# Another order of work at the end of each layer of a two-layer graph attention kernel

## The chip, the cores and the metric

One core of a Trainium2 chip runs the whole kernel. The metric is the device time of one execution in microseconds (us); less is better. The time before is the median of three runs; one more execution was profiled, and every row quoted here comes from that one. Engines are named as in the profile: PE (TensorE), DVE (VectorE), ACT (ScalarE), POOL (GpSimd) and SP (SyncE). Each engine works through its own list of instructions in order and waits on semaphores for the others.

## The reference, cut to what matters

Two graph attention layers over 6250 nodes with 256 features and 200000 edges, sorted by their destination. Layer 0 has four heads, layer 1 has one. For each layer:

```
te  = relu(edge_attr @ We + be) * exp(x @ Wo + bo)[src]      # edge features
hx  = x @ Wg                                                # node rows
al  = leaky_relu(a_s.hx[src] + a_d.hx[dst] + a_e.(te @ Wge))  # one logit per edge and head
m   = segment_max(al, dst);  p = exp(al - m[dst])
out = segment_sum(p * hx[src], dst) / segment_sum(p, dst) + b
```

Every node also has a loop to itself, whose edge feature is the mean of those that come in. Layer 0 adds its input and a Relu, layer 1 adds its input and the features from ahead of both layers.

## The kernel before, in words

**Tiling.** The edges are cut into 1563 chunks of 128, and these into 66 superchunks per layer: 64 of 24 chunks, then one of 14 and one of 13 (`cuts`, line 47). Edges are sorted, so a superchunk covers at most 112 neighbouring nodes, and its sums are one PSUM tile of 128 rows.

**A superchunk's steps**, with the methods that issue them:

- `gather` (L866): POOL issues one indirect DMA for each chunk (L873), which fetches 128 rows of the layer's node table into G.
- `spread`, `parts`, `blocks` (L981, L1012, L1033): DVE prepares the destination's term of the logits; `blocks` writes the block product aq (L1037).
- `rphase1` (L948) is a generator: for each half of the features PE multiplies (L964) and ACT applies the Relu (L967 or L969). `rphase2` (L978) and `adst` (L1044) add both terms in PSUM (zad); `edge_rows` (L1047) transposes them on DVE.
- `logits` (L1064): DVE adds the gathered terms (L1072 is the first instruction that needs the gathers) and scans for segment maxima (L1087, L1089). `ends` transposes the scans' ends on PE (L1100), `links` (L1102) scans them on DVE (L1110, L1112) and transposes back on PE (L1117).
- `maxima` (L1119): DVE forms the maxima (L1127 to L1147), ACT the Exp (L1146), DVE stores the weights (L1150). `scale` (L1174) multiplies G by them on DVE (L1181). `carried` (L1155) adds the open row of the superchunk before, from its evicted sums U, to G.
- `onehots` (L1001) builds the one-hot matrix S on DVE (L1009). `sums` (L1185) multiplies S and G chunk by chunk on PE (L1193) into u, and `evict` (L1195) copies u to U on ACT (L1198).
- `finish` (L1311): the merge with the loop to itself, `merge` (L1200) and the rest of `nodes0` or `nodes1` (L1246, L1300). It is a generator as well, so its steps can be set singly between others. In layer 1 its last two steps (L1306, L1308) write the result row fb.
- In layer 0 `rows1` (L1286 on PE, L1288 on ACT), `rows2` (L444 on PE) and `rows3` (L448 on DVE, L1298 on ACT, a write by SP, L1327) make layer 1's table row. In layer 1 `rows3` alone writes fb out: by SP (L1332), and by a POOL scatter (L1335) for the last two superchunks.

**Order.** The order of issue is the order in which these methods are called; no scheduler moves them. `edges` (L637) calls them for each superchunk, with the next superchunk's features between. The last three of each layer, called a, b and c here (24, 14 and 13 chunks), are issued by `ending` (L736), once per layer. `pv` is the superchunk ahead of a, `late` the one before that, and `after` the first superchunk of the next layer, or nothing in layer 1. At the end of layer 0, `gather(after)` reads the table that a, b and c have just written; it waits for the last write. Buffers that bound the order: U has three buffers, S, fb and the table row two, u, y and zad in PSUM one each.

Of the kernel before, what the change touches and what calls it, by code (L numbers as in the profile page):

```python
# [32 lines left out]
C = 24  # L33
# [46 lines left out]
class Kernel:  # L80
# [655 lines left out]
    def ending(self, a, b, c, pv, late, after):  # L736

        nc, k = self.nc, a["k"]
        self.load_lb(k + 3)
        self.load_lb(k + 4)  # L740
        self.gather(b)
        self.gather(c)
        for q in () if after else (b, c):
            q["idx"] = idx = self.np_.tile([P, 1], I32, name="oidx")
            nc.vector.tensor_add(idx, self.base_f[:, q["s"]:q["s"] + 1], self.iota_m)
            nc.vector.memset(idx[0:1, :], 1 << 20)
        drain(self.logits(a))
        self.ends(a)
        self.spread(b)
        self.parts(b)  # L750
        y = self.rphase1(b)
        next(y)
        self.links(a)
        self.rows2(late)
        self.load_fl(k + 1)
        self.blocks(b)
        drain(self.maxima(a))
        drain(y)
        self.load_ea(k + 2)
        self.rphase2(b)  # L760
        self.adst(b)
        drain(self.scale(a))
        self.carried(a)
        n = a["C"]
        self.sums(a, (0, n // 2))
        self.rows3(late)
        self.edge_rows(b)
        self.onehots(b)
        drain(self.logits(b))
        self.ends(b)  # L770
        self.rows1(pv)
        self.spread(c)
        self.parts(c)
        self.sums(a, (n // 2, n - n // 4))
        self.links(b)
        self.sums(a, (n - n // 4, n))
        self.load_fl(k + 2)
        self.rows2(pv)
        y = self.rphase1(c)
        next(y)  # L780
        self.blocks(c)
        drain(self.maxima(b))
        self.evict(a)
        drain(y)
        self.load_ea(k + 3)
        self.rphase2(c)
        self.adst(c)
        self.rows3(pv)
        n = b["C"]
        drain(self.scale(b, cuts=(1, 1 + n // 2, n)))  # L790
        drain(self.scale(b, cuts=(0, 1)))
        self.carried(b)
        self.onehots(c)
        f = self.finish(a)
        if after:
            for _ in range(9):
                next(f)
        else:
            drain(f)
            self.rows3(a)  # L800
        m = c["C"]
        self.sums(b, (1, n - 3))
        self.edge_rows(c)
        drain(self.logits(c))
        self.ends(c)
        for _ in range(3):
            next(f, None)
        self.links(c)
        self.sums(b, (n - 3, n), (0, 1))
        self.load_fl(k + 3)  # L810
        drain(f)
        self.evict(b)
        if after:
            self.rows1(a)
            self.rows2(a)
        drain(self.maxima(c))
        y = self.rphase1(after) if after else iter(())
        next(y, None)
        drain(self.scale(c, cuts=(1, 1 + m // 2, m)))
        drain(self.scale(c, cuts=(0, 1)))  # L820
        self.carried(c)
        self.sums(c, (1, m), (0, 1))
        if after:
            self.rows3(a)
        f = self.finish(b)
        while after and "hw" not in b:
            next(f)
        if not after:
            drain(f)
            self.rows3(b)  # L830
        self.evict(c)
        drain(f)
        drain(y)
        self.rows1(b)
        self.rows2(b)
        f = self.finish(c)
        while after and "hw" not in c:
            next(f)
        if after:
            self.rows3(b)  # L840
        drain(f)
        self.rows1(c)
        self.rows2(c)
        self.rows3(c)
        if after:
            self.gather(after)
            self.nodes(after)
            self.spread(after)
            self.parts(after)
            self.blocks(after)  # L850
            self.rphase2(after)
            self.adst(after)
            self.edge_rows(after)
            self.onehots(after)
# [602 lines left out]
def drain(g):  # L1457
    for _ in g:
        pass
# [93 lines left out]
```

## Time and profile before

| what | value |
|---|---|
| median of 3 runs (lowest to highest) | 4082.15 us (4076.27 to 4089.95) |
| profiled execution | 4081.92 us, its span 4080.1 us |
| busy over the span: PE, DVE, ACT, POOL | 3031.4, 2850.5, 520.3, 3008.6 us |
| ending of layer 0, 2009 to 2084 (75 us): PE, DVE, ACT, POOL busy | 53.0, 55.2, 12.6, 23.8 us |
| ending of layer 1, 4009 to 4081 (72 us): PE, DVE, ACT, POOL busy | 40.9, 39.7, 5.1, 26.2 us |

A row of the timeline reads: start in us from the span's start, duration in us, engine, line of the kernel, operation, output<-inputs, partitions x elements, count, and in brackets how long the engine stood idle before it and what ended that. Neighbouring instructions of one line are merged into one row with their count. A row of a source line reads: count, shortest/median/longest duration in ns, first and last start in us. The chain of waits is followed back from the last instruction; its shares are those of the span.

### The profile page before, as it was taken

Reading aid. Unit: us, or ns where it says so; the run is one execution under the profiler, and the core shown is the slowest. Engines: PE = TensorE matmul, PEld = TensorE weight load, DVE = VectorE, ACT = ScalarE, POOL = GpSimd, SP = SyncE. Lnnn points to the kernel's source line nnn. Section 1 sums busy time; section 2 is a strip of 40 time slices with the busy share of each in tenths; the row PEclk is TensorE's granted clock in tenths of the full one; section 3 lists DMA queues with packets and bytes.
Section 4 is the critical chain, followed back from the end, with each engine's and each line's share of the span. In section 5 each row is a group of like instructions: output and inputs, shape, how many; then the busy total and the mean of one; then the engine's idle time right before and its main releaser. Section 6 shows DMA issues by size and latency. Waiting matters only on the chain.

```text
span 4080.1 us, 34027 instructions
## 1 busy us (share of the span) xinstructions
PE 3031.4 (74%) x9878; PEld 1887.7 (46%) x9878; DVE 2850.5 (70%) x6188; ACT 520.3 (13%) x1162; POOL 3008.6 (74%) x3255
## 2 busy tenths in 40 slices
PE   8878778777877878878756767767677677676776
PEld 6555444444444544544534444444444444444444
DVE  7898777877877877778755656656566565665665
ACT  5111111111111111111110000000000000000000
POOL 6677777777777777777747777777777777777774
PEclk9787777777777777877767777777777777777777
DMA  7455555555555555455434454454445445445542
GB/s 254 130 151 140 144 150 142 144 150 139 146 150 140 145 149 147 140 148 148 134 99 131 138 142 134 139 142 140 135 138 140 135 138 144 131 138 143 141 133 81
DMA packets 231086, 576.17 MB, mean 141 GB/s; under 512 B 63098, under 2 KB 87872, under 8 KB 230826
## 3 DMA queue, kind: packets, MB, share of 16 engines
q0 software_dynamic: 150144, 422.75, 38.9%
q1 hardware_dynamic: 80331, 150.52, 11.5%
q8 instruction: 79, 1.29, 0.1%
q14 instruction: 116, 0.94, 0.1%
q10 hardware_dynamic: 416, 0.67, 0.1%
HBM read 542.72 MB, written 31.09 MB: 141 GB/s over the span
## 4 chain that ended last, share of the span: by engine, by line
POOL 33%; DVE 31%; issue 13%; PE 12%; DMA 8%; ACT 2%; DVEq 0%; SPq 0%; ACTq 0%; POOLq 0%
POOL G L873 33%; DVE G L1181 11%; DMA G<-T,src 7%; PE y L964 6%; DVE S L1009 6%; PE u L1193 2%; DVE rt L1058 2%; DVE lb L993 1%; ACT R L969 1%; PE ps L444 1%; PE zad L978 1%; DVE G L1163 1%; DVE ade L1061 1%; DVE al L1076 1%; DVE al L1074 1%
## 5 line engine op out<-in xcount | busy, mean ns | idle before, releaser
L873 POOL DMA_INDIRECT G<-T,src x3102 | 2956.6, 953 | 1010.5 <-issue 912.6
L1193 PE MATMUL u<-G,S 128*128 128x270 f32 (+1 forms) x6252 | 1474.8, 396 | 113.8 <-DVE G L1171 109.2
L1193 PEld LDWEIGHTS u<-G,S 128*128 128x128 f32 x6252 | 1199.2, 194 | 396.0 <-DVE G L1171 172.7
L1181 DVE TENSOR_TENSOR G<-G,kps 128x6144 f32<-128x6144 f32 (+2 forms) x140 | 853.3, 6100 | 0.0
L964 PE MATMUL y<-ea,webd 64*128 64x384 f32 (+1 forms) x1056 | 729.5, 840 | 68.7 <-ACT R L969 66.9
L1100 PE MATMUL lf<-ident,fb 128*36 128x128 f32 (+1 forms) x132 | 49.8, 377 | 674.1 <-DVE fb L1089 647.6
L1072 DVE TENSOR_TENSOR G<-rt,G 128x96 f32<-128x96 f32 (+1 forms) x132 | 30.4, 230 | 715.5 <-DMA G<-T,src 714.8
L978 PE MATMUL zad<-R,wea 128*64 128x384 f32 (+1 forms) x1056 | 469.7, 804 | 1.5 <-ACT R L969 1.2
L964 PEld LDWEIGHTS y<-ea,webd 64*128 64x128 f32 x1056 | 294.3, 307 | 317.2 <-issue 191.3
L1009 DVE TENSOR_TENSOR S<-kps,loc 128x3072 f32<-128x3072 f32 x132 | 437.6, 3315 | 4.6
L969 ACT ACTIVATE R<-y,webd 128x768 f32<-128x768 f32 x260 | 233.2, 897 | 1523.5 <-PE lf L1117 1130.1
L1100 PEld LDWEIGHTS lf<-ident,fb 128*36 128x36 f32 (+1 forms) x132 | 15.6, 118 | 716.1 <-DVE fb L1089 688.7
L978 PEld LDWEIGHTS zad<-R,wea 128*64 128x64 f32 x1056 | 158.2, 206 | 315.9 <-issue 208.7
L1127 DVE TENSOR_TENSOR fb<-flpen,lf 128x192 f32<-128x192 bf16 (+1 forms) x132 | 36.7, 278 | 237.7 <-PE lf L1117 237.7
L1030 PE MATMUL zad<-a,Q 128*128 128x12 bf16 (+1 forms) x132 | 25.8, 196 | 155.8 <-DVE a L1025 155.8
L1058 DVE STREAM_TRANSPOSE rt<-zad 128x768 f32<-128x768 f32 (+1 forms) x130 | 124.8, 960 | 9.5 <-PE zad L1044 8.9
L444 PE MATMUL fin<-wg,h1T 128*128 128x260 f32 x264 | 129.0, 640 | 2.0 <-ACT h1T L1288 2.0
L1198 ACT ACTIVATE U<-u 128x270 f32<-128x270 f32 (+1 forms) x132 | 51.8, 393 | 500.6 <-PE u L1193 500.6
L993 DVE TENSOR_TENSOR lb<-lb,kps 128x1536 bf16<-128x1536 bf16 (+1 forms) x68 | 113.6, 1670 | 0.0
L444 PEld LDWEIGHTS fin<-wg,h1T 128*128 128x128 f32 x264 | 72.4, 302 | 48.3 <-issue 33.9
L1030 PEld LDWEIGHTS <-Q 128*128 128x128 bf16 x132 | 16.0, 121 | 169.2 <-DVE a L1025 162.6
L1223 ACT ACTIVATE mw<-mw,mg 128x2 f32<-128x2 f32 x66 | 19.7, 298 | 576.2 <-DVE mg L1222 576.2
(191 smaller groups left out, 2160.9 us busy)
## 6 DMA issues: line engine op xcount, KB each, us to landing
G<-T,src POOLq DMA_INDIRECT x3102, 2.8
ea<-in_ea_dram SPq DMA_DIRECT2D x64, 768.0 KB
lb<-locrow SPq DMA_DIRECT2D x64, 384.0 KB
T<-t1row SPq DMA_DIRECT2D x66, 227.5 KB
tw<-T SPq DMA_DIRECT2D x66, 225.8 KB
tw<-T SPq DMA_DIRECT2D x66, 117.2 KB
tw<-in_x_dram SPq DMA_DIRECT2D x66, 112.0 KB
out_dram<-fb SPq DMA_DIRECT2D x64, 112.0 KB
```

Source lines behind the costliest of these rows:

```text
L444: self.nc.tensor.matmul(ps[:, :L.MW], hT[:, k, :], self.wg[L.l][:, k, :], start=(k == 0), stop=(k == 1))
L873: nc.gpsimd.indirect_dma_start(out=G[:, c, 0:L.TW], out_offset=None, in_=self.rows[L.l][0:n * (1 + L.l), :], in_offset=bass.IndirectOffset ...
L964: nc.tensor.matmul(y[:, o], self.webd[l][r, :], ea[r, w], start=True, stop=True)
L969: nc.scalar.activation(R[:, i, :32 * c].rearrange("p (b n) -> p b n", b=2), y.rearrange("p (b n) -> p b n", b=2)[:, :, :16 * c], AF.Relu, ...
L978: nc.tensor.matmul(st["zad"][i * PH:(i + 1) * PH, o], self.wea[l][0], R[:, i, w], start=True, stop=False)
L993: V.tensor_tensor(lb[:, :, :n], lb[:, :, :n], self.k_part.unsqueeze(2).to_broadcast([P, i, n]), op=OP.is_equal)
L1009: nc.vector.tensor_tensor(st["S"][:, c0:c1, :], self.k_iota.unsqueeze(1).to_broadcast(w), self.loc[:, o + c0:o + c1].unsqueeze(2).to_broad ...
L1058: V.transpose(rv[:, :32 * c].rearrange("p (b n) -> p b n", b=2), z.rearrange("p (b n) -> p b n", b=2)[:, :, :16 * c])
L1100: self.nc.tensor.transpose(self.lf[0:e.shape[1], 1:P + 1], e, self.ident)
L1181: nc.vector.tensor_tensor(v, v, pw[:, c0:c1, :].unsqueeze(3) .to_broadcast([P, c1 - c0, H, L.F]), op=OP.mult)
L1193: nc.tensor.matmul(st["u"][:, :L.W], S[:, i, :], G[:, i, 0:L.W], start=(j == 0), stop=(j == c - 1))
L1198: self.nc.scalar.activation(U[:, :L.W], st["u"][:, :L.W], AF.Copy)
```

## The change

All of it lies in `ending`, so it acts once in each layer. Nothing is computed otherwise; the instructions are the same in number and shape, and their order changes:

- a's sums are cut after 8 and 12 of 24 chunks instead of after 12 and 18; the transposes of b's logits and of b's links stand at the cuts.
- b's maxima, a's eviction and b's scaling move ahead of c's edge features (`rphase1(c)`, `blocks(c)`). Before, maxima and eviction stood behind the first half of these, the scaling behind all of them.
- a's merge: four steps stay where nine (layer 0) or all (layer 1) stood; three follow behind c's `ends`, one behind the last of b's sums, the rest after c's carried row.
- c's maxima move ahead of b's eviction.
- In layer 0 a's table rows (`rows1`, `rows2`, `rows3`) move from before c's maxima to behind c's eviction. In layer 1 a's result is written after c's sums are issued.

```
         n = a["C"]
-        self.sums(a, (0, n // 2))
+        self.sums(a, (0, n // 3))
...
-        self.sums(a, (n // 2, n - n // 4))
+        self.sums(a, (n // 3, n // 2))
         self.links(b)
-        self.sums(a, (n - n // 4, n))
+        self.sums(a, (n // 2, n))
         self.load_fl(k + 2)
         self.rows2(pv)
+        drain(self.maxima(b))
+        self.evict(a)
+        n = b["C"]
+        drain(self.scale(b, cuts=(1, 1 + n // 2, n)))
+        drain(self.scale(b, cuts=(0, 1)))
         y = self.rphase1(c)
         next(y)
         self.blocks(c)
-        drain(self.maxima(b))
-        self.evict(a)
         drain(y)
         self.load_ea(k + 3)
         self.rphase2(c)
         self.adst(c)
         self.rows3(pv)
-        n = b["C"]
-        drain(self.scale(b, cuts=(1, 1 + n // 2, n)))
-        drain(self.scale(b, cuts=(0, 1)))
         self.carried(b)
         self.onehots(c)
         f = self.finish(a)
-        if after:
-            for _ in range(9):
-                next(f)
-        else:
-            drain(f)
-            self.rows3(a)
+        for _ in range(4):
+            next(f)
         m = c["C"]
         self.sums(b, (1, n - 3))
         self.edge_rows(c)
         drain(self.logits(c))
         self.ends(c)
         for _ in range(3):
-            next(f, None)
+            next(f)
         self.links(c)
         self.sums(b, (n - 3, n), (0, 1))
         self.load_fl(k + 3)
-        drain(f)
+        next(f)
+        drain(self.maxima(c))
         self.evict(b)
-        if after:
-            self.rows1(a)
-            self.rows2(a)
-        drain(self.maxima(c))
         y = self.rphase1(after) if after else iter(())
         next(y, None)
         drain(self.scale(c, cuts=(1, 1 + m // 2, m)))
         drain(self.scale(c, cuts=(0, 1)))
         self.carried(c)
+        drain(f)
         self.sums(c, (1, m), (0, 1))
+        f = self.finish(b)
         if after:
+            while "hw" not in b:
+                next(f)
+        else:
             self.rows3(a)
-        f = self.finish(b)
-        while after and "hw" not in b:
-            next(f)
-        if not after:
             drain(f)
             self.rows3(b)
         self.evict(c)
+        self.rows1(a)
+        self.rows2(a)
         drain(f)
+        if after:
+            self.rows3(a)
         drain(y)
         self.rows1(b)
         self.rows2(b)
```

## The prediction

> **What bounds the kernel now.** I read the page first, for the chain that ended last, then the instructions of the gather line in layer 1.
>
> ```profile
> span 4080.1 us, 34027 instructions
> POOL 33%; DVE 31%; issue 13%; PE 12%; DMA 8%; ACT 2%; DVEq 0%; SPq 0%; ACTq 0%; POOLq 0%
> POOL G L873 33%; DVE G L1181 11%; DMA G<-T,src 7%; PE y L964 6%; DVE S L1009 6%; PE u L1193 2%; DVE rt L1058 2%; DVE lb L993 1%; ACT R L969 1%; PE ps L444 1%; PE zad L978 1%; DVE G L1163 1%; DVE ade L1061 1%; DVE al L1076 1%; DVE al L1074 1%
> L873 POOL DMA_INDIRECT G<-T,src x1563: 942/946/1172, 2083.6 to 4039.9; - x196
> ```
>
> Layer 1 runs from its first gather at 2083.6 to its last at 4039.9: 1563 gathers in 1956.3 us are 1.25 each, which is one gather's 0.95 plus 0.30 of issue. POOL never pauses for long, so all of layer 1 hangs on the moment of its first gather, and what the change saves ahead of it arrives at the end whole. The change touches only the two endings (about 2009 to 2084 and 4009 to 4081), some 3.6% of the span; the other 96% I leave as it is. a, b and c are the last three superchunks (24, 14 and 13 chunks; a chunk's sum is two matmuls). Times are us from the span's start, and "now" is the kernel before.
>
> **Layer 1's ending, up to c's gathers.** The timeline, in order:
>
> ```profile
> 4022.36 7.85 PE L1193 MATMUL u<-G,S 128*128 128x261 f32 x24 [2.99 <-DVE G L1171]
> 4022.36 0.95 POOL L873 DMA_INDIRECT G<-T,src  x1 [0.30 <-issue]
> 4026.41 0.18 DVE L1072 TENSOR_TENSOR G<-rt,G 128x14 f32<-128x14 f32 x1 [1.19 <-DMA G<-T,src]
> 4027.38 0.20 DVE L1089 TENSOR_TENSOR_SCAN fb<-pen,al 128x14 f32<-128x14 bf16 x1
> 4030.18 2.89 PE L1193 MATMUL u<-G,S 128*128 128x261 f32 x12
> 4033.28 0.18 DVE L1127 TENSOR_TENSOR fb<-flpen,lf 128x28 f32<-128x28 bf16 x1 [1.80 <-PE lf L1117]
> 4033.87 0.20 DVE L1140 TENSOR_SCALAR mt<-lf,m 1x1 f32<-1x1 f32 x1
> 4037.08 0.76 ACT L967 ACTIVATE R<-y,webd 128x224 f32<-128x224 f32 x2 [20.00 <-PE y L964]
> 4037.72 0.19 ACT L1146 ACTIVATE kps<-mt 128x15 f32<-128x15 f32 x1
> 4038.03 4.01 DVE L1181 TENSOR_TENSOR G<-G,kps 128x1792 f32<-128x1792 f32 x3
> 4038.78 1.52 PE L978 MATMUL zad<-R,wea 128*64 128x224 f32 x8
> 4039.86 0.95 POOL L873 DMA_INDIRECT G<-T,src  x1 [0.30 <-issue]
> 4040.43 4.59 PE L1193 MATMUL u<-G,S 128*128 128x261 f32 x20
> ```
>
> - The cut of a's sums at 8 chunks instead of 12. b's scan (L1089) is done at 4027.58, but its transpose queues behind 24 matmuls until 4030.2. The last 8 of these run at the pace of the next row (2.89 / 12 = 0.24), so 16 end near 4028.3. The transposes go there; four chunks more (1.9) end at 4030.4, and L1117 lets L1127 start at 4030.7 instead of 4033.28: 2.6 earlier. PE does the same matmuls without a gap, so a's sums end, and c's edge features begin, where they do now.
> - b's maxima and scaling ahead of c's edge features. Now b's Exp (L1146) is ready at 4033.87 + 0.20 = 4034.07, but ACT holds c's first Relu (L967), which waits 20 us for PE; the Exp starts at 4037.72: 3.65 lost. In the new order it follows L1127 by 0.8, at 4031.5, on an idle ACT. Scaling starts 0.31 after it and takes 4.01: 4031.8 to 4035.8 instead of 4042.04.
> - What stands behind it. c's block product (L1037, 0.2) now waits on DVE for that scaling: done at 4036.0. PE first needs it at L978, 4038.78, so 2.7 of slack hides it; without slack each us late would cost one. a's eviction now precedes c's Relu on ACT, at a's last sum (4030.2 and two stretches of 2.9: near 4036.1), and its 0.4 lies under the matmuls of c's first half (the Relu starts at 4037.08). So b's sums start at 4040.43 as now, and ten chunks end at 4045.0. This edit alone is worth nothing on PE; it empties DVE.
> - DVE then: carried row 0.6, one-hots of c 2.0, four steps of a's merge 0.8 (all lengths of now), done near 4040.3; c's transposes and reduce follow its features (4040.7) until 4041.9.
>
> c's logits have to wait for c's own gathers. b shows the lag: last gather 4022.36 + 0.95, logits at 4026.41, 3.1 later. c's last ends at 4040.81, so its logits start at **4043.9**.
>
> **Layer 1's ending, from c's logits on.**
>
> ```profile
> 4048.67 0.18 DVE L1072 TENSOR_TENSOR G<-rt,G 128x13 f32<-128x13 f32 x1 [0.18 <-issue]
> 4049.85 0.42 PE L1100 MATMUL lf<-ident,fb 128*33 128x128 f32 x1 [4.83 <-DVE fb L1089]
> 4051.61 0.18 DVE L1127 TENSOR_TENSOR fb<-flpen,lf 128x26 f32<-128x26 bf16 x1 [0.41 <-PE lf L1117]
> 4054.96 0.39 ACT L1198 ACTIVATE U<-u 128x261 f32<-128x261 f32 x1 [9.04 <-PE u L1193]
> 4055.24 0.18 ACT L1146 ACTIVATE kps<-mt 128x14 f32<-128x14 f32 x1
> 4055.54 3.74 DVE L1181 TENSOR_TENSOR G<-G,kps 128x1536 f32<-128x1536 f32 x3
> 4057.39 7.64 PE L1193 MATMUL u<-G,S 128*128 128x261 f32 x26 [2.47 <-issue]
> 4059.86 0.20 DVE L1214 SCALAR_TENSOR_TENSOR mg<-U,cnt,tw 128x1 f32<-128x1 f32 x1
> 4062.30 0.48 DVE L1308 SCALAR_TENSOR_TENSOR fb<-tw,mw,fb 128x256 f32<-128x256 f32 x1
> 4065.07 0.39 ACT L1198 ACTIVATE U<-u 128x261 f32<-128x261 f32 x1 [4.04 <-PE u L1193]
> 4068.72 1.00 POOL L1335 DMA_INDIRECT out_dram<-fb,oidx  x1 [4.63 <-DVE flag_i L864]
> ```
>
> - Logits: 4048.67 becomes 4043.9, 4.77 earlier. The transpose follows 1.18 later, at 4045.1, just behind b's ten chunks (4045.0). The three steps of a's merge placed here run in PE's shadow; the fourth (L1306, 0.48) overlaps L1117, costing about 0.05. L1127 at 4046.85.
> - c's Exp: 0.8 later, 4047.65. Now it starts at 4055.24, because b's eviction (4054.96) stands ahead of it on ACT; the change swaps them. **7.6 earlier.** Scaling starts at 4047.95 and b's eviction goes beside it.
> - c's sums start at 4057.39 - 7.6 = 4049.8. Their 26 matmuls take 7.64, though 20 took 4.59 before: at 0.22 more for each, 26 are 5.91. The 1.73 between are matmuls on the halved clock after PE stood still for 2.47. In the new order b's last chunks (1.9) end near 4048.5, and the still stretch before c's is 1.3. I take the full pace: the last sum ends at 4055.7, eviction 9.3 earlier than 4065.07. Bounds: 7.6 (as slow as now) to 9.3; I take **9.3**.
> - DVE's queue in that stretch: c's scaling to 4051.7, carried row 0.55, the rest of a's merge (L1308, 0.5), then b's merge (4059.86 to 4062.78: 2.9) to 4055.7, just when U of c arrives (4056.1). It is hidden by 0.4; if c's sums got faster yet, b's merge would be next. SP's write of a goes out at 4052.8 instead of 4047.7 and POOL's scatter of b at 4055.8; in this ending neither queue has anything behind them but c's scatter. From c's eviction to the last scatter (4068.72) and the end nothing is changed.
>
> **Layer 0's ending.** The same steps with four heads, then the tables of layer 1:
>
> ```profile
> 2046.28 5.27 PE L1193 MATMUL u<-G,S 128*128 128x270 f32 x20
> 2054.90 0.40 PE L1100 MATMUL lf<-ident,fb 128*36 128x128 f32 x1 [3.35 <-DVE fb L1089]
> 2056.26 0.42 DVE L1266 TENSOR_TENSOR fa<-tw,mw 128x256 f32<-128x256 f32 x1
> 2058.76 0.26 DVE L1127 TENSOR_TENSOR fb<-flpen,lf 128x104 f32<-128x104 bf16 x1
> 2061.31 0.22 ACT L1146 ACTIVATE kps<-mt 128x56 f32<-128x56 f32 x1
> 2061.69 3.74 DVE L1181 TENSOR_TENSOR G<-G,kps 128x1536 f32<-128x1536 f32 x3
> 2064.02 6.19 PE L1193 MATMUL u<-G,S 128*128 128x270 f32 x26
> 2070.25 0.40 ACT L1198 ACTIVATE U<-u 128x270 f32<-128x270 f32 x1 [1.47 <-PE u L1193]
> 2072.96 1.15 PE L444 MATMUL fin<-wg,h1T 128*128 128x260 f32 x4 [0.89 <-ACT h1T L1288]
> 2076.07 0.42 ACT L1272 ACTIVATE fb<-fb 128x256 f32<-128x256 f32 x1 [1.26 <-DVE fb L1270]
> 2077.76 2.10 PE L444 MATMUL fin<-wg,h1T 128*128 128x260 f32 x4 [0.53 <-ACT h1T L1288]
> 2083.62 0.94 POOL L873 DMA_INDIRECT G<-T,src  x1 [43.94 <-DMA T<-t1row]
> ```
>
> - b's ten chunks end at 2051.55. By the steps of layer 1, half a us longer for four heads, DVE has c's scans ready some 2 us before that, and c's gathers have landed long before; so the transpose moves from 2054.90 to 2051.5. L1127 now stands behind a's merge (from 2056.26) and follows 3.86 later; in layer 1 the same pair is 1.76 apart. I take 1.65: 2053.15.
> - Exp: now 2.55 after L1127, behind b's eviction and a's table rows on ACT, both moved away. Bounds 0.8 (layer 1) and 2.55; 1.3 for four heads: 2054.45, 6.85 earlier. c's scaling runs 2054.85 to 2058.6 (now to 2065.43).
> - What is given back. DVE is the path from there: now 10.64 from the end of scaling to c's Relu (2076.07). The rest of a's merge comes into it: 2.5 (L1266 to L1127) and three small steps, 3.1. Without a wait the Relu comes at 2058.6 + 10.64 + 3.1 = 2072.35, 3.7 earlier.
> - New waits. c's eviction stands on ACT behind the Exp of b's merge: 2058.6 + carried row 1.0 + 3.1 + 1.45 + 0.8 on ACT, 2065.0, still ahead of 2070.25. a's table rows follow it there: eviction and transposed copy 0.8, four matmuls of L444 1.15, half of the next features 1.6, their Relu 0.9, b's copy 0.4, the Exp of c's merge 0.2: 2070.05. DVE is there at 2058.6 + 1.0 + 3.1, b's merge 4.85, a's L448 0.35 and the first 1.45 of c's merge: 2069.35. So 0.7 is lost: 2073.05, 3.0 earlier. With b's L444 on the slow clock (2.10 for 1.15) DVE waits 0.95 more: 2.1 earlier. With a's L444 and the features slow as well nothing is left (+0.2). Bounds -3.7 and +0.2; I take the middle of the two likely ones, **2.5**. The first gather of layer 1 moves from 2083.62 to 2081.1, and layer 1 with it.
>
> The Trainium skill (TensorE: Matmul & The Clock Gate, "What's actually happening") says that PE falls to half clock after an idle window of about 3.4 us. By that rule c's sums in layer 1 would keep the full clock for certain, and the 1.73 would be sure. The trace differs: 2.47 idle sufficed at 4057.39.
>
> **Sum.** 9.3 + 2.5 = 11.8, from the profiled execution's 4081.92 (span 4080.1): **4070.1**. The median of the runs is 4082.15, 0.2 above that execution, so the change reads as 0.29%. A measurement tells about 0.3% (12.2 us) of this kernel from nothing, so the forecast lies on the edge of what shows as faster.
>
> **Rivals.**
> - *Slow clock in c's last sums* (0.14). For it: 4057.39 was slow after 2.47 of standing still; against: that stretch halves. Layer 1 gives 7.6, in all 4071.8.
> - *Layer 0 yields nothing* (0.18). The three pieces above are slow: PE stands still for over 2 us between them, and L444 did run slow at 2077.76. Only layer 1's 9.3 is left: 4072.6. The Trainium skill (same section) says that the clock's windows run free of the kernel's start, so which pieces are slow would change from run to run; one trace cannot show that.
> - *The change does not do what it says* (0.04): b's Exp stays at 4037.7 through a wait that I missed. Then scaling ends at 4042.0, the block product at 4042.2 makes c's features 3.4 late and b's ten chunks end at 4048.4. Taken in both endings, layer 1 keeps 5.9 and layer 0 loses 0.9: 4076.9.
> - *Slower: a's buffers* (0.04). a's result row is now written out later, and c's merge reuses its buffer: in layer 0 the write leaves near 2068.0 and c needs the buffer near 2072.4, in layer 1 near 4052.8 and 4057.9. From the end of L444 (2079.86) to 2083.62 is 3.76 with such a write in it, so it should fit into 4.4 and 5.1. Above 4.4 each us is paid in layer 0, above 5.1 in layer 1 too; from 10.7 the gain is eaten, and at 18 it is 13.6 + 12.9 - 11.8 lost: 4096.6.
>
> **How the numbers follow.** Forecast 0.60, by its own bounds 4069 to 4074. The runs of the kernel before spread from 4076.27 to 4089.95, so a median of three moves by some 4; that and the first two rivals make 4062.5 to 4078.0 for eight in ten. Faster by over 0.3%: half of the forecast (0.30) and a third of the first two rivals (0.11), 0.41. Slower: the last rival, 0.04. Within 0.3%: the rest, 0.55.
>
> **What would show it.** Layer 1: b's Exp within 1 us of L1127; c's logits waiting on the gathers' landing; c's Exp before b's eviction; the last 26 sums in about 5.9. Layer 0: first gather near 2081. Wrong if c's features wait for L1037, if c's eviction in layer 0 comes later than 2068, or if a write of a's row holds c's merge.

## The result

| | median of runs, us | profiled execution's span |
|---|---|---|
| before | 4082.33 (4076.27 to 4089.95, 9 runs) | 4080.1 |
| changed | 4069.42 (4067.02 to 4074.25, 9 runs) | 4069.1 |

The ratio is 0.9968, with an interval at 95% of 0.9958 to 0.9978: the change takes 12.9 us off, and the interval reaches from 9 to 17. The two profiled executions differ by 11.0. In the changed kernel every line from about 860 on has a number two lower than before (L1193 is L1191, L1146 is L1144).

### The profile page after: what moved, and what is told of

Same layout as the page of the kernel before. It is cut to its first block, busy times and chain, and to the rows that moved or that the text cites. A ratio compares the mean times of both kernels' runs of the same rounds, so it can differ in the third digit from the quotient of the medians.

```text
span 4069.1 us, 34027 instructions
## 1 busy us (share of the span) xinstructions
PE 3035.0 (75%) x9878; PEld 1880.9 (46%) x9878; DVE 2850.1 (70%) x6188; ACT 520.3 (13%) x1162; POOL 3007.7 (74%) x3255
## 3 DMA queue, kind: packets, MB, share of 16 engines
q8 instruction: 79, 1.29, 0.1%
## 4 chain that ended last, share of the span: by engine, by line
POOL 32%; DVE 31%; PE 13%; issue 12%; DMA 9%; ACT 2%; DVEq 0%; SPq 0%; POOLq 0%; ACTq 0%
POOL G L871 32%; DVE G L1179 11%; DMA G<-T,src 9%; PE y L962 7%; DVE S L1007 6%; DVE rt L1056 2%; PE u L1191 2%; PE zad L976 2%; DVE lb L991 1%; ACT R L967 1%; PE ps L444 1%; DVE ade L1059 1%; DVE m L1130 1%; DVE al L1074 1%; DVE G L1161 1%
## 5 line engine op out<-in xcount | busy, mean ns | idle before, releaser
L1191 PE MATMUL u<-G,S 128*128 128x270 f32 (+1 forms) x6252 | 1457.5, 392 | 97.9 <-DVE G L1169 94.5
L1191 PEld LDWEIGHTS u<-G,S 128*128 128x128 f32 x6252 | 1185.7, 192 | 378.3 <-DVE G L1169 160.0
L962 PE MATMUL y<-ea,webd 64*128 64x384 f32 (+1 forms) x1056 | 739.4, 850 | 68.6 <-ACT R L967 66.8
L1098 PE MATMUL lf<-ident,fb 128*36 128x128 f32 (+1 forms) x132 | 49.8, 377 | 671.6 <-DVE fb L1087 643.7
L962 PEld LDWEIGHTS y<-ea,webd 64*128 64x128 f32 x1056 | 296.9, 310 | 320.2 <-issue 197.0
L1125 DVE TENSOR_TENSOR fb<-flpen,lf 128x192 f32<-128x192 bf16 (+1 forms) x132 | 36.6, 277 | 241.6 <-PE lf L1115 241.4
L444 PE MATMUL fin<-wg,h1T 128*128 128x260 f32 x264 | 133.1, 657 | 3.3 <-ACT h1T L1286 3.3
L444 PEld LDWEIGHTS fin<-wg,h1T 128*128 128x128 f32 x264 | 74.5, 311 | 51.8 <-issue 35.5
```

The source lines that it names most:

```text
L444: self.nc.tensor.matmul(ps[:, :L.MW], hT[:, k, :], self.wg[L.l][:, k, :], start=(k == 0), stop=(k == 1))
L962: nc.tensor.matmul(y[:, o], self.webd[l][r, :], ea[r, w], start=True, stop=True)
L1098: self.nc.tensor.transpose(self.lf[0:e.shape[1], 1:P + 1], e, self.ident)
L1191: nc.tensor.matmul(st["u"][:, :L.W], S[:, i, :], G[:, i, 0:L.W], start=(j == 0), stop=(j == c - 1))
```

## The profile after the change

The page, its first line and the chain of work that ended last; then the row of the gather line in layer 1 (duration shortest/median/longest, first and last start):

```profile
span 4069.1 us, 34027 instructions
...
POOL 32%; DVE 31%; PE 13%; issue 12%; DMA 9%; ACT 2%; DVEq 0%; SPq 0%; POOLq 0%; ACTq 0%
POOL G L871 32%; DVE G L1179 11%; DMA G<-T,src 9%; PE y L962 7%; DVE S L1007 6%; DVE rt L1056 2%; PE u L1191 2%; PE zad L976 2%; DVE lb L991 1%; ACT R L967 1%; PE ps L444 1%; DVE ade L1059 1%; DVE m L1130 1%; DVE al L1074 1%; DVE G L1161 1%
```

```profile
L871 POOL DMA_INDIRECT G<-T,src x1563: 942/946/1179, 2081.5 to 4037.8; - x196
```

The chain is what it was: POOL's gathers, 1563 of them in 1956.3 us again. They begin 2.1 earlier (2081.5 for 2083.6) and end 2.1 earlier, and the rest of the 11.0 comes after the last one. So one subtraction splits the change in two: up to the first gather of layer 1 it is layer 0's ending, behind the last gather layer 1's.

The timeline of the changed kernel in layer 1's ending (start, length, engine, line, operation, and in brackets the idle time before it with what ended it):

```profile
4020.11 6.78 PE L1191 MATMUL u<-G,S 128*128 128x261 f32 x16 [2.98 <-DVE G L1169]
4029.08 0.18 DVE L1125 TENSOR_TENSOR fb<-flpen,lf 128x28 f32<-128x28 bf16 x1 [1.14 <-PE lf L1115]
4029.96 0.19 ACT L1144 ACTIVATE kps<-mt 128x15 f32<-128x15 f32 x1 [15.13 <-DVE mt L1138]
4030.27 4.00 DVE L1179 TENSOR_TENSOR G<-G,kps 128x1792 f32<-128x1792 f32 x3
...
4034.20 0.17 DVE L1035 TENSOR_TENSOR aq<-zad,quad 128x12 bf16<-128x12 f32 x1
...
4037.22 1.53 PE L976 MATMUL zad<-R,wea 128*64 128x224 f32 x8
...
4037.84 0.94 POOL L871 DMA_INDIRECT G<-T,src  x1 [0.30 <-issue]
...
4038.87 4.59 PE L1191 MATMUL u<-G,S 128*128 128x261 f32 x20
...
4040.91 0.18 DVE L1070 TENSOR_TENSOR G<-rt,G 128x13 f32<-128x13 f32 x1 [0.92 <-DMA G<-T,src]
...
4043.30 0.27 PE L1098 MATMUL lf<-ident,fb 128*33 128x128 f32 x1
...
4045.06 0.18 DVE L1125 TENSOR_TENSOR fb<-flpen,lf 128x26 f32<-128x26 bf16 x1
...
4045.93 0.18 ACT L1144 ACTIVATE kps<-mt 128x14 f32<-128x14 f32 x1 [7.13 <-DVE mt L1138]
...
4046.81 0.39 ACT L1196 ACTIVATE U<-u 128x261 f32<-128x261 f32 x1 [0.69 <-PE u L1191]
...
4048.09 5.96 PE L1191 MATMUL u<-G,S 128*128 128x261 f32 x26 [1.32 <-ACT U L1196]
...
4054.08 0.39 ACT L1196 ACTIVATE U<-u 128x261 f32<-128x261 f32 x1 [1.89 <-PE u L1191]
...
4057.73 1.00 POOL L1333 DMA_INDIRECT out_dram<-fb,oidx  x1 [2.48 <-DVE flag_i L862]
```

Read it against the rows of the prediction after taking 2.02 off each of those (the last gather's start: 4039.86, now 4037.84). b's Exp stood at 4035.70 on that scale and is at 4029.96, right behind L1125. c's logits (4040.91) now wait 0.92 for the landing of c's gathers; they stood at 4046.65. c's transpose (4043.30) starts as b's ten chunks end (4038.87 + 4.59 = 4043.46, an end that the profile models). c's Exp is ahead of b's eviction and 7.29 earlier; c's 26 matmuls take 5.96 instead of 7.64, behind a stillness of 1.32 instead of 2.47; c's eviction is 8.97 earlier, and so is the last scatter.

Layer 0's ending in the changed kernel, same view:

```profile
2051.51 0.27 PE L1098 MATMUL lf<-ident,fb 128*36 128x128 f32 x1
...
2053.06 0.26 DVE L1125 TENSOR_TENSOR fb<-flpen,lf 128x104 f32<-128x104 bf16 x1
...
2054.45 0.22 ACT L1144 ACTIVATE kps<-mt 128x56 f32<-128x56 f32 x1 [3.92 <-DVE mt L1142]
...
2056.68 6.16 PE L1191 MATMUL u<-G,S 128*128 128x270 f32 x26 [0.16 <-issue]
...
2064.49 0.37 ACT L1196 ACTIVATE U<-u 128x270 f32<-128x270 f32 x1
...
2065.19 1.15 PE L444 MATMUL fin<-wg,h1T 128*128 128x260 f32 x4 [2.12 <-ACT h1T L1286]
...
2066.26 2.29 PE L962 MATMUL y<-ea,webd 64*128 64x384 f32 x4
...
2069.82 2.10 PE L444 MATMUL fin<-wg,h1T 128*128 128x260 f32 x4 [0.64 <-ACT h1T L1286]
2069.89 0.16 DVE L1235 TENSOR_TENSOR mg<-U,mw 128x4 f32<-128x4 f32 x1 [0.85 <-ACT mw L1233]
...
2071.95 0.43 DVE L448 TENSOR_TENSOR t1row<-fin,bias 128x260 f32<-128x260 f32 x1 [1.29 <-PE fin L444]
...
2073.76 0.42 DVE L1276 TENSOR_TENSOR t1row<-tw,hw 128x256 f32<-128x256 f32 x1
2073.88 0.42 ACT L1270 ACTIVATE fb<-fb 128x256 f32<-128x256 f32 x1 [1.26 <-DVE fb L1268]
...
2081.45 0.95 POOL L871 DMA_INDIRECT G<-T,src  x1 [41.66 <-DMA T<-t1row]
```

c's transpose is 3.4 earlier, c's Exp 6.9, c's sums 7.3, c's eviction 5.8, c's Relu (L1270) 2.2, the first gather 2.2. The gain shrinks from step to step. DVE now carries the rest of a's merge between c's scaling and that Relu, and two rows show waits on top of it: 0.85 for the Exp of c's merge, which stands on ACT behind the Relu of the next features (L962 took 2.29, part of it at half clock), and 1.29 for b's L444, which took 2.10 where a's took 1.15.

## The experiments

A difference of two us is below what these times tell apart, so the runs are read by two distances in their traces, both counted from a's first sum (the group of L1191, L1193 before, that opens each ending): in layer 0 to the first gather of layer 1, in layer 1 to the span's end. The expectations of e1 to e8 count layer 1 from the last gather instead. That did not carry over: these runs were on three chips (14 for e1 to e4, 5 for e5 to e11, 7 for e12), on which the kernel before takes 4736 to 4792 us and the last gather starts some 2.2 ahead of a's first sum (17.5 behind it in the profile before), so that gathers do not bind in the ending. To compare, add 17.5 to a distance that is counted from the last gather; a first gather at 2083.6 is a distance of 57.1 in layer 0.

| run | layer 0 | layer 1 | sum against the old order | median against before, us | ratio, interval at 95% |
|---|---|---|---|---|---|
| before, first profile | 57.14 | 57.79 | | | |
| changed, first profile | 54.80 | 48.97 | -11.5 | -12.9 | 0.9958 to 0.9978 |
| e1, new order in layer 1 only | 57.67 | 48.27 | -9.3 | -12.4 | 0.9966 to 0.9985 |
| e2, new order in layer 0 only | 54.27 | 57.89 | -3.1 | -7.1 | 0.9973 to 0.9992 |
| e3, b ahead only | 53.34 | 52.25 | -9.7 | -10.4 | 0.9968 to 0.9987 |
| e4, Exp of c first only | 57.86 | 54.85 | -2.5 | -3.3 | 0.9985 to 1.0004 |
| e5, all but b ahead and the cuts | 54.32 | 53.21 | -7.7 | -5.2 | 0.9980 to 1.0008 |
| e6, eviction of b first | 54.60 | 52.55 | -8.1 | -9.4 | 0.9969 to 0.9995 |
| e7, old cuts | 54.14 | 49.28 | -11.8 | -13.2 | 0.9965 to 0.9989 |
| e8, split | 55.05 | 46.56 | -13.6 | -16.2 | 0.9958 to 0.9982 |
| e9, early features | 54.91 | 48.26 | -12.1 | -13.5 | 0.9964 to 0.9986 |
| e10, split and early features | 52.81 | 46.63 | -15.8 | -16.2 | 0.9952 to 0.9978 |
| e11, changed kernel again | 53.78 | 49.76 | -11.7 | -14.5 | 0.9961 to 0.9982 |
| e12, table rows between | 52.58 | 46.39 | -16.3 | -16.9 | 0.9950 to 0.9977 |

"Old order" is the mean of the four distances with it (57.14 and 57.67 in layer 0, 57.79 and 57.89 in layer 1: 115.25 in all). The changed order gave 53.8 to 54.8 in layer 0 (the changed kernel, e2, e11) and 48.3 to 49.8 in layer 1 (the changed kernel, e1, e9, e11). That is the scatter from one trace to the next: 1.0 in layer 0 and 1.5 in layer 1. A smaller difference between two single traces says nothing by itself, unless their rows show step by step where it comes from.

### e1 and e2: which layer

The ending twice in the class, the new order in one layer and the old in the other:

```
    def ending(self, a, b, c, pv, late, after):
-       ...
+       (self.ending0 if after else self.ending1)(a, b, c, pv, late, after)
```

> The new order in layer 1's ending alone, the old one in layer 0. Two distances are read from the trace: the start of layer 1's first gather (2083.62 before, 2081.45 after) and the distance from the last gather's start to the span's end (40.24 before, 31.26 after). Theory (the endings add up, and layer 0 is worth 2.2): first gather at 2083.6, distance 31.3, some 9 us less in all. Rival (layer 0 gives nothing, what its anchor shows is chance): the same distance, and the whole gain of some 11 to 13 us here. Rival (layer 1 gains only because layer 0 hands its work over in another state): distance above 35.

> The new order in layer 0's ending alone. Theory: first gather of layer 1 at 2081.5 (2083.62 before), the distance from the last gather to the end 40.2 as before, some 2.2 us less, which the time itself can hardly show. Rival (layer 0 yields nothing): first gather at 2083.6 or later.

e1's timeline in layer 1, and e2's in layer 0 (each kernel holds two endings, so its lines are some 120 higher):

```profile
4674.30 5.47 PE L1314 MATMUL u<-G,S 128*128 128x261 f32 x16 [2.99 <-DVE G L1292]
...
4701.41 5.96 PE L1314 MATMUL u<-G,S 128*128 128x261 f32 x26 [1.32 <-ACT U L1319]
```

```profile
2391.87 6.44 PE L1314 MATMUL u<-G,S 128*128 128x270 f32 x16 [2.09 <-DVE G L1292]
...
2446.14 0.94 POOL L994 DMA_INDIRECT G<-T,src  x1 [58.86 <-DMA T<-t1row]
```

e1 has a span of 4722.6: layer 1's ending takes 48.3 with the new order and 57.9 with the old (e2). In e2 the first gather comes 2446.14 - 2391.87 = 54.27 behind a's first sum; e1 has 57.67 with the old order. So by the distances the endings add up, layer 1 is worth some 9 and layer 0 some 3, and the rival by which layer 0 yields nothing is out. The gain of layer 1 is much the same where gathers do not bind (9.6 here, 8.8 in the first two profiles), which the prediction had them do. The times agree for e1 only: e2's interval is 3.8 to 12.8 us and leaves out its 3.1. The distances leave out the rest of the kernel, and no run shows where that difference comes from.

### e3, e4, e5, e6: the parts of the change one by one

e3 is the kernel before with one block moved, and the new cuts of a's sums:

```
+       drain(self.maxima(b)); self.evict(a)
+       drain(self.scale(b, cuts=(1, 1 + n // 2, n))); drain(self.scale(b, cuts=(0, 1)))
        y = self.rphase1(c)
...
-       drain(self.maxima(b)); self.evict(a)
...
-       drain(self.scale(b, cuts=(1, 1 + n // 2, n))); drain(self.scale(b, cuts=(0, 1)))
```

> Only b's maxima, eviction of a and scaling of b move ahead of c's edge features (with the cuts of a's sums); a's merge stays in one piece ahead of c's logits, and c's Exp stays behind b's eviction. Theory (the move alone empties DVE, since the whole merge of 2.9 fits before c's gathers have landed; the swap of Exp and eviction is worth about 1.2 more): c's logits about 0.5 later than in the changed kernel, at 3.6 after the last gather's start, their transpose still where b's ten chunks end; c's Exp 1.2 later than in the changed kernel; distance from the last gather to the end 32.5 if c's sums run at full clock, 34.2 if the stillness of some 2.5 ahead of them halves it. Layer 0: first gather between 2080.5 and 2082. Rival (what frees DVE is that the merge is spread between the waits): c's logits stay more than 4 after the changed kernel's, distance 36 or more.

e4 is the kernel before with c's maxima, and with them c's Exp, ahead of b's eviction (in layer 0 also ahead of a's table rows); e6 is the changed kernel with the eviction in front again:

```
        drain(f)
+       drain(self.maxima(c))
        self.evict(b)
...
-       drain(self.maxima(c))
```

> Only one step is taken from the change: c's maxima and Exp go ahead of b's eviction; everything else as before. Theory: in layer 1 the Exp follows L1127 by 0.8 as it does in the changed kernel (3.6 now), but b's sums are as late as before, and c's sums must wait for b's eviction: they start 2.0 earlier, with a stillness of 0.5 ahead of them, hence at full clock (5.9 instead of 7.64): distance from the last gather to the end 36.5. If the stillness is not what halves the clock: 38.2. Layer 0: about 1 earlier. Rival (the swap is worth nothing while b's eviction holds the sums): distance 40.

> The changed kernel with b's eviction ahead of c's maxima again. Theory: the Exp of c waits for the eviction, 1.2 later in layer 1 and 1.0 in layer 0; c's sums begin 1.1 later, after a stillness of 2.4: distance from the last gather to the end 32.4 at full clock, 34.1 if the stillness halves it; first gather of layer 1 near 2082.4. Rival (in the changed kernel the sums are held by the eviction anyway, so the swap no longer matters): 31.3 and 2081.5.

e5 is the changed kernel with that block in its old places. It also has the old cuts of a's sums, which its expectation counts as kept; so e3 and e5 split the change into two halves with nothing in common:

```
-       drain(self.maxima(b)); self.evict(a)
-       drain(self.scale(b, cuts=(1, 1 + n // 2, n))); drain(self.scale(b, cuts=(0, 1)))
        y = self.rphase1(c)
...
        self.blocks(c)
+       drain(self.maxima(b)); self.evict(a)
        drain(y)
...
        self.rows3(pv)
+       drain(self.scale(b, cuts=(1, 1 + n // 2, n))); drain(self.scale(b, cuts=(0, 1)))
```

> The change without its first half: b's maxima and scaling stay between the halves of c's edge features and behind them, all else as in the changed kernel (merge spread, Exp ahead of eviction, cuts). Theory (the parts overlap, they do not add up): in layer 1 b's Exp stays where it was (behind c's first Relu), c's logits come 2.0 earlier than before, c's sums about 4.4 earlier and at full clock: distance from the last gather to the end 34 to 36 (40.24 before, 31.26 after). Rival (the move of b is what the gain hangs on): 38 or more. Rival (the move of b is worth nothing, as it is worth nothing on PE): 31.3.

c's 26 matmuls in layer 1, from the timelines of e3, e4, e6 and e11, the changed kernel run again:

```profile
4707.20 7.65 PE L1193 MATMUL u<-G,S 128*128 128x261 f32 x26 [2.47 <-issue]
```

```profile
4710.73 5.99 PE L1193 MATMUL u<-G,S 128*128 128x261 f32 x26 [0.48 <-ACT U L1198]
```

```profile
4758.80 7.64 PE L1191 MATMUL u<-G,S 128*128 128x261 f32 x26 [2.47 <-issue]
```

```profile
4757.66 5.96 PE L1191 MATMUL u<-G,S 128*128 128x261 f32 x26 [1.32 <-ACT U L1196]
```

The first of c's logits in layer 1, from the timelines of e4 and e5:

```profile
4703.66 0.18 DVE L1072 TENSOR_TENSOR G<-rt,G 128x13 f32<-128x13 f32 x1 [0.17 <-issue]
```

```profile
4753.09 0.18 DVE L1070 TENSOR_TENSOR G<-rt,G 128x13 f32<-128x13 f32 x1 [0.18 <-issue]
```

Three things follow.

- The halved clock of c's sums in layer 1 is shown from both sides. With 2.47 of stillness ahead of them the 26 matmuls take 7.64 or 7.65 (before, e2, e3, e6); with 1.32 or 0.48 they take 5.96 to 5.99 (the changed kernel, e1, e4, e7 to e12). e5 stands apart, with 6.51 behind 0.48: there the clock was down already. The swap of c's Exp and b's eviction is what shortens the stillness. Set e6, without it, beside e11, the changed kernel: up to c's transpose the two traces agree (24.05 and 24.03 from a's first sum); then e6 has c's Exp 1.17 later, its sums 1.68 longer, and the end 2.8 later. In layer 0 the swap shows nothing: e6's 54.60 lies within the changed order, where 55.9 was expected.
- What the merge of a, spread between the waits, is worth in layer 1 depends on b's scaling. With b ahead it does nothing: e3 keeps the merge in one piece and e6 spreads it, both evict b ahead of c's Exp, and they stand at 52.25 and 52.55. With b left back, e4 has it in one piece and e5 spreads it: c's logits come 26.97 and 24.66 behind a's first sum, 2.3 earlier, and the end 1.6 earlier. In layer 0 e3 has 53.34, less than every trace with the full change; the section on the prediction takes this up.
- The parts do not add up. In layer 1, moving b ahead alone gives 5.6 (57.84 to 52.25), all the rest without it 4.6 (e5), and together they give 8 to 9.6. In layer 0 they give 4.1 and 3.1 alone, and together 2.6 to 3.6. Both bring the same event forward, the start of c's sums (35.0 from a's first sum in layer 1 before, 29.9 in e3, 31.8 in e5, 28.0 together). e4 gives 3.0 in layer 1 and, where about 1 was expected, nothing in layer 0, where a's transposes, a's table rows and the next features still stand on PE ahead of c's sums. e5 lies within its expectation in layer 1 (53.2 in 51.5 to 53.5), and e3, e4 and e6 come out later than theirs: e3 by 0.55 and e6 by 0.95 of the branch with the halved clock (51.7 and 51.6), e4 by 0.85 of the branch at full clock (54.0), each on the branch that its sums took. In layer 0 e3 gained more than expected (53.34, where 54.0 to 55.5 was set).

### e7: does the cut of a's sums matter?

```
-       self.sums(a, (0, n // 3))
+       self.sums(a, (0, n // 2))
...
-       self.sums(a, (n // 3, n // 2))
+       self.sums(a, (n // 2, n - n // 4))
...
-       self.sums(a, (n // 2, n))
+       self.sums(a, (n - n // 4, n))
```

> The changed kernel with the old cuts of a's sums (a half, a quarter, a quarter). Theory: b's links come 1.2 later in layer 0 and 2.6 later in layer 1, which the slack of c's block product (2.7 in layer 1) just covers: distance 31.3 to 31.6, first gather near 2081.5. Rival (b's scaling is on the path to c's features): the distance grows by up to 2.6, to 33.9.

Layer 1 of e7, DVE's block product and PE's first use of it:

```profile
4744.93 0.17 DVE L1035 TENSOR_TENSOR aq<-zad,quad 128x12 bf16<-128x12 f32 x1
...
4745.32 1.52 PE L976 MATMUL zad<-R,wea 128*64 128x224 f32 x8
```

The product is done 0.22 before PE would start the group; in the changed kernel 4037.22 - 4034.37 = 2.85 before. The distance is within the scatter (49.28). So the cut is a reserve of 2.6, and gains nothing by itself.

### e8, e9, e10, e12: is there a version that beats both?

e8 takes three chunks of b's sums from ahead of c's transpose:

```
-       self.sums(b, (1, n - 3))
+       self.sums(b, (1, n - 6))
...
+       self.sums(b, (n - 6, n - 4))
        self.links(c)
-       self.sums(b, (n - 3, n), (0, 1))
+       self.sums(b, (n - 4, n), (0, 1))
...
-       drain(self.scale(c, cuts=(1, 1 + m // 2, m)))
+       drain(self.scale(c, cuts=(1, 3, 1 + m // 2, m)))
```

> The changed kernel with three more chunks of b's sums moved from ahead of c's transpose: two of them between it and c's links, one behind, and c's scaling cut so that two chunks are ready first. Theory (in the changed kernel c's transpose waits for b's ten chunks, 1.0 in layer 1 and 1.5 in layer 0, and PE then stands still for 1.0 and 1.3): distance from the last gather to the end 29.8, first gather of layer 1 near 2080.5. Rival (c's gathers' landing or DVE's scaling binds just behind): no change, 31.3 and 2081.5.

Layer 1 came out better than expected: 46.56, which is 1.7 to 3.2 less than the changed order gave. Layer 0 did not: c's eviction comes 37.2 behind a's first sum (38.5 in e11), but the first gather at 55.05. The timeline of e8 shows why, the next features and then b's L444:

```profile
2455.97 2.93 PE L963 MATMUL y<-ea,webd 64*128 64x384 f32 x4
...
2460.16 2.10 PE L444 MATMUL fin<-wg,h1T 128*128 128x260 f32 x4 [0.65 <-ACT h1T L1287]
```

Both ran at half clock; e11, the changed kernel on the same chip, has the features in 1.55 and b's L444 in 1.14. What was gained ahead of the eviction was lost to the clock behind it. e9 therefore moves the features to where PE stands still for 2.1, and e11 is the changed kernel again as a yardstick:

```
        self.rows1(a)
+       drain(y)
        self.rows2(a)
...
-       drain(y)
        self.rows1(b)
```

> The changed kernel with the second half of the next layer's first features (L962) put right behind a's transposes in layer 0's ending, into the 2.12 for which PE stands still there, instead of behind a's L444. Distances are now counted from a's first sum: to the first gather of layer 1 (57.14 before, 54.80 in the changed kernel, 54.27 to 55.05 in the runs so far that have its order there), and to the span's end in layer 1 (57.79 before, 48.97 changed). Theory (the features stand between a's L444 and b's transposes at a moment when PE's clock falls): c's eviction stays at 38 to 39 from a's first sum, the three L444 run in 1.14 each or nearly, and the first gather comes at 52 to 53; layer 1 unchanged at 48.3 to 49. Rival (the table rows wait on DVE anyway): first gather at 54 to 55.

> The changed kernel itself, on the chip of the two runs above, as their yardstick. Theory: layer 1 at 48.3 to 49.3 from a's first sum to the end, layer 0 at 54 to 55, some 11 us less than the kernel before whatever the chip's own time. Rival (what the change is worth hangs on gathers that bind the ending, which they did not on the chips of the runs so far): below 6 us.

The yardstick came out close to the theory, 0.2 below its range in layer 0 and 0.5 above it in layer 1 (53.78 and 49.76); the rival that gathers must bind is out. e9 is a miss: 54.91. Its timeline behind a's L444, b's transposes and b's L444:

```profile
2462.92 0.41 PE L1284 MATMUL fin<-ident,fb 128*128 128x128 f32 x2 [1.54 <-DVE cnt L1207]
2463.86 2.10 PE L444 MATMUL fin<-wg,h1T 128*128 128x260 f32 x4 [0.53 <-ACT h1T L1286]
```

a's L444 did run in 1.14. But the hole did not go, it moved. b's transposes reuse the accumulator that a's L448 frees, and DVE reaches that line only after b's merge; where the features stood, they had filled that wait, and PE's clock had stayed up. Now PE stands still for 1.54 there, and b's L444 takes 2.10.

> The early features together with the split of b's sums. In the split alone layer 0 had c's eviction 1.8 earlier but the first gather 0.8 later, the features having run at half clock (2.93). Theory: with the features early the 1.8 arrive: first gather at 50.5 to 52 from a's first sum; layer 1 as in the split alone, 46.6: in all some 4 to 5 us less than the changed kernel, 15 to 17 less than before. Rival (the clock falls somewhere else in layer 0's tail and eats it): first gather at 54 or later.

Together the two edits give 52.81 and 46.63. In layer 0 that is 2.2 less than e8 but only 1.0 less than the yardstick, which is the scatter, and it misses the 50.5 to 52 expected: b's transposes still stand still for 1.54, and b's L444 takes 1.60. e12 adds the last step, the table rows of a and b (L448) ahead of the wait:

```
        self.rows2(a)
-       drain(f)
        if after:
+           for _ in range(4):
+               next(f)
            self.rows3(a)
+       drain(f)
...
        if after:
+           for _ in range(4):
+               next(f)
            self.rows3(b)
```

> The split and the early features, and in layer 0 the table rows of a and of b (L448) put after the fourth step of the next merge that follows the scaled rows (behind L1268) instead of behind or ahead of it. What it tells apart: with the early features alone, b's transposes stood still for 1.54 although their input was ready 0.9 before, since they reuse the accumulator that a's L448 frees. Theory (that wait and the wait of c's merge for b's L444 are what is left): b's transposes 0.9 earlier than in the run before (counted from c's eviction), c's merge no longer waits for b's L444, first gather of layer 1 at 50.5 to 51.7 from a's first sum (52.81 in the run with split and early features); layer 1 at 46.6. Rival (the clock of the L444 decides alone): 52.8 as before.

The timeline of e12, b's transposes, b's L444 and c's Relu:

```profile
2424.39 0.44 PE L1289 MATMUL fin<-ident,fb 128*128 128x128 f32 x2 [0.65 <-ACT fb L1275]
...
2425.36 1.14 PE L444 MATMUL fin<-wg,h1T 128*128 128x260 f32 x4 [0.53 <-ACT h1T L1291]
...
2429.07 0.42 ACT L1275 ACTIVATE fb<-fb 128x256 f32<-128x256 f32 x1 [1.94 <-DVE fb L1273]
```

The waits went as expected: b's transposes come 2.5 behind c's eviction (3.4 in e10), b's L444 is fast, and DVE no longer waits for it. Yet the first gather moves only 0.2, to 52.58. DVE is now the path: from c's eviction to that Relu it works through both merges with no wait over 0.3. That DVE would bind right behind the waits, and keep the gain to 0.2, the theory had not seen.

e12 has the lowest ratio of all: 0.9963 of the kernel before (0.9950 to 0.9977), 16.9 us. By the distances it is 4.6 ahead of the changed kernel; the times cannot separate it from the changed kernel, e8 or e10, since the intervals overlap. One cost in layer 0 no version takes off, c's own L444: it took 1.70 to 2.10 in all 14 traces (2.10 in e12, behind 3.04 of stillness ahead of c's transposes), where the others got down to 1.14.

## Why the prediction came out

The forecast was 4070.1 by a sum of 11.8; the distances say 11.2 in the first two profiles, the medians 12.9. That the median lies 0.7 from the forecast is luck in part, since its interval is some 4 us wide to either side. The steps say more:

- **b's maxima and scaling ahead of c's features.** Forecast: b's Exp within 1 of L1127, 2.7 of slack behind the block product. Measured: 0.88 and 2.85, and e7 spends all but 0.22 of that slack. That the edit "alone is worth nothing on PE; it empties DVE" holds as a mechanism, but it hid the weight: e3 shows that this edit is the largest of all, 5.6 in layer 1.
- **b's sums start as now.** They start 0.46 later on the last gather's scale. The first 16 matmuls took 6.78, at half clock throughout, where I had reckoned 5.9, by taking the last 8 of the row of 24 off at full pace.
- **c's logits.** I took 3.1 from the end of the last gather to its use; it was 2.13 (4040.91 against 4038.78). The 3.1 was a misreading: the last 13 gathers are c's, so b's last starts at 4023.61 and not at 4022.36, and b's lag was 1.85. It changed nothing, since c's transpose stands behind b's ten chunks, a bound that the prediction had put only 0.1 away; that this error cost nothing was luck.
- **c's Exp ahead of b's eviction, and the clock.** Forecast 7.6 and 5.91, measured 7.29 and 5.96; eviction 9.3 forecast, 8.97 measured. The bet was on the clock, with 1.7 at stake: the trace before had shown one slow group, and e3 and e6 now show both sides of it.
- **Layer 0.** c's transpose, L1127 and the Exp came within 0.1 of the forecast, c's eviction 0.5 earlier. The new waits were 0.85 and 1.29 for my 0.7 and 0.95. In all 2.17 for 2.5. e2 and e11 with the same order, and e7 but for the cuts, have 3.1 to 3.6 against the mean of the old order. All of these lie within the bounds (-3.7 to +0.2), and the clock of eight matmuls decides within them: from c's eviction to the first gather the first profile takes 16.97 and e11 15.25, and that is the 0.74 by which the next features ran longer (2.29, 1.55) and the 0.96 of b's L444 (2.10, 1.14).
- **The rivals.** Slow sums: not here, but e6 shows the price (1.7, as set). Layer 0 yields nothing: refuted by e2. The change does not do what it says: refuted by b's Exp. a's buffers: c's write into the table row (L1276 at 2073.76) starts with no wait, so the later write of a held nothing.
- **What I did not see.** Spreading a's merge adds nothing in layer 1 once b is ahead, and in layer 0 it gives back nearly 3. The prediction had counted this as 3.1, but not asked what the ending would be without it. e3 is the nearest run to that; it also has c's Exp and a's table rows in their old places. c's scaling and c's Relu in layer 0, from e3 and from e11:

```profile
2423.60 3.74 DVE L1181 TENSOR_TENSOR G<-G,kps 128x1536 f32<-128x1536 f32 x3
...
2438.09 0.42 ACT L1272 ACTIVATE fb<-fb 128x256 f32<-128x256 f32 x1 [1.26 <-DVE fb L1270]
```

```profile
2442.23 3.74 DVE L1179 TENSOR_TENSOR G<-G,kps 128x1536 f32<-128x1536 f32 x3
...
2459.58 0.42 ACT L1270 ACTIVATE fb<-fb 128x256 f32<-128x256 f32 x1 [1.26 <-DVE fb L1268]
```

From one to the other DVE needs 14.49 in e3 and 17.35 in e11. So 2.86 is given back, for the 3.1 of the prediction, while c's scaling starts 2.41 later in e3 (31.28 behind a's first sum, for 28.87). The difference, 0.45, is what e3 gains on e11 (53.34 for 53.78). That is one trace of each; against the other two traces of the changed order e3 is 0.9 and 1.5 ahead. How much of that would repeat, and what the spread merge alone is worth in layer 0, stays open.

## What to carry to other kernels

Where several edits pull the same instruction out of the same queue, try each alone: the sum of their single gains was half as much again as what they gave together (9.7 and 7.7 against 11.5), and one of them, the spread merge, brought c's logits 2.3 forward without its neighbour and added nothing with it. A gap on PE has to be judged by what runs behind it: filling one gap opened the next, and the half clock there ate the gain. And read small gains by distances between anchors in the trace that the rest of the kernel cannot move; for one order they agreed with each other to 1.5 us, where the interval of a median reached 6.7 to either side. They do not speak for the rest of the kernel, as e2 shows.

## What the runs showed of the hardware

PE's clock: behind a stillness of 2.47 the 26 matmuls of c's sums took 7.64 or 7.65 in four traces of four, behind 1.32 or 0.48 they took 5.96 to 5.99 in nine of ten. The slow group is not slow throughout. In e6 its first matmuls follow each other at 0.22, the next eight at some 0.43, the rest at 0.22 again. The Trainium skill (TensorE: Matmul & The Clock Gate, "What's actually happening") puts the fall at an idle window of about 3.4; here 2.47 sufficed.

The profile's record of the granted clock shows how. In each of the 14 traces its changes lie a whole number of steps of 3.41 us apart. In e6 one step runs from 4756.13 to 4759.54 and holds the whole 2.47: PE is busy for 0.28 of it, and the next step, to 4762.95, has half clock. In e11 the 1.32 leaves the step from 4756.02 at 0.61, and the clock stays. The four slow groups all have a step of 0.28. Over all steps at full clock, PE was busy for at least 0.41 of every one that another followed; of the 2101 that a half one followed, 95 in 100 had 0.43 or less. So it is the busy share of a step that tells, more than one unbroken stillness. Busy time alone does not settle it: in layer 0 of e6, 26 matmuls took 7.85 behind 1.07 and a step of 0.69, of which some two thirds were the next features, matmuls with 64 rows. And a step at half clock reaches on into what follows: in layer 1 of e5 the 26 took 6.51 behind 0.48, after eight that were slow already. Whether a stillness of 2.47 that straddles two steps would lower the clock, no run shows.

The kernel before took 4082 us in the first measurement and 4736 to 4792 on chips 14, 5 and 7; no chip number was kept for the first, so that it was another one is inferred from the times. The change's ratio was alike (0.9968, and 0.9971 in e11). In e11 layer 1's 1563 gathers span 2467.14 to 4726.68, 1.45 each instead of 1.25, though most follow each other at 1.25 there too: 63 gaps of more than 2 us, 6.1 on average, make the difference. The timeline of e11 in the middle of layer 1 shows PE handing out single matmuls 2.8 apart:

```profile
3530.66 0.60 PE L1191 MATMUL u<-G,S 128*128 128x261 f32 x1 [2.43 <-issue]
3533.46 0.60 PE L1191 MATMUL u<-G,S 128*128 128x261 f32 x1 [2.20 <-issue]
3536.28 0.59 PE L1191 MATMUL u<-G,S 128*128 128x261 f32 x1 [2.23 <-issue]
```

The profile names no engine that they wait for ("issue"). None of this stands inside the two endings, and its cause stays open.
